# Head stage of a two-layer graph kernel: tap steps, forward transforms, statistics and norms put in another order, the last block's second sums moved to VectorE

## The chip, the cores and the metric

The kernel runs on one core of a Trainium2 chip. The metric is the device time of one execution in microseconds. The engines of the core run side by side, each through its own list of instructions: TensorE (PE in the profile, its weight loads PEld), VectorE (DVE), ScalarE (ACT), GpSimd (POOL) and SyncE (SP), which here only issues DMAs.

## The reference, cut to what matters

Two graph layers act on 128 graphs of 128 nodes with 256 channels, in float32. The stage that the change touches computes the first convolution path of layer 0: layer norm, ReLU, a 1x1 convolution (conv1), and the first half of a 17-tap convolution (conv2) over the node axis.

```python
# layer 0
h = jnp.maximum(_layernorm(x, axis=-1), 0.0)
x = x + _L0_gnn_ref(h, adj, L0_gnn_w_se, L0_gnn_b_se, L0_gnn_conv1_w)
...
def _L0_gnn_ref(x, mask, w_se, b_se, conv1_w):
    xc = jnp.transpose(x, (0, 2, 1))
    h = _bn(_conv1d(xc, conv1_w, 0), bn1_g, bn1_b, bn1_m, bn1_v)
    h = jax.nn.relu(h)
    h = _bn(_conv1d(h, conv2_w, 8), bn2_g, bn2_b, bn2_m, bn2_v)
    x_conv = jnp.transpose(jax.nn.relu(h + xc), (0, 2, 1))
    s = x @ w_se.T + b_se
    sq = jnp.sum(s * s, axis=-1)
    dist = sq[:, :, None] + sq[:, None, :] - 2.0 * jnp.einsum('bnd,bmd->bnm', s, s)
    A = jnp.exp(-dist) * mask
    msg = jax.nn.relu(x @ w_msg.T + b_msg)
    x_nmp = jnp.einsum('bnm,bmd->bnd', A, msg)
    ...
```

(The argument lists are shortened.) Behind it come a GRU cell on `x_conv`, `x_nmp` and x, and layer 1: two graph convolutions on each of five groups of nodes, added up.

## The kernel before

Conv2 is done in the frequency domain. The 128 graphs are dealt into 32 blocks (`NBLK`) of four (`BB`). The program has three stages. The **head stage** (about 0 to 254 us of the span) transforms conv2's taps and, block by block, conv1's output. The **spectral stage** (to about 430 us) multiplies the two spectra, 68 frequencies. The rest, nearly 1400 us, does the inverse transform, the message passing, the gates and layer 1.

The head stage runs under a manual schedule: on every engine the instructions stand in the order in which the Python code calls them. The later stages are ordered by the framework's planner. The pieces of the head stage, with their lines:

- `head_load(i)` (L198): SP issues the DMA of block i of x into a tile `ln`, of which there are four. It is called for block i+4 at the start of iteration i.
- `head_stats(i, parts)` (L208, L209, L212, L214): VectorE takes mean and variance of two graphs a part, by two bn_stats and two bn_aggr; behind the second part it adds the epsilon, and GpSimd takes the power of -1/2 into `rs`.
- `head_norm(i, wk, on_act)` (L221, L224, L227): VectorE makes `nm` = -mean x rs, then ScalarE normalises the first `on_act` graphs of the block in place, VectorE the others.
- `head_turn(i)` (L237, L238, L239): TensorE transposes the block, eight transposes into two PSUM banks; ScalarE applies ReLU into the tile `ht`, 512 columns at a time; SP writes `ht` to DRAM (`htd`).
- `head_conv1(i, h)` (L251, L254): one half of conv1 of a block, four matmuls of 128x256 (eight records in the trace) into one bank; VectorE evicts it with the batch norm's shift as a maximum, into `h1`.
- `head_sums(i, h)` (L261 to L263): GpSimd's sum and difference of two mirrored halves of the nodes, and an added constant: even and odd part, for a shorter transform.
- `head_spectra(X, i)` (L279, L288, L290): the forward transform of a block: TensorE in tiles of 64x64 into four banks; ScalarE and VectorE copy two banks each into `X`.
- a **tap step** (`between()`, which is `some_spectra`, one chunk of `weight_spectra`; L180, L187, L189): TensorE multiplies taps with the transform's matrix, in row tiles of 17, for two or three columns into four banks; ScalarE copies three or four of the banks, VectorE the fourth where the chunk has three columns. A set of taps has three chunks, 16 sets are done. Behind each set SP writes its spectrum to DRAM (L191, `vd<-sp`) and loads the taps after the next (L166, `w<-in_w2t_dram`); these two are issued at the call that begins the next set.

PSUM's eight banks are taken in turn: each new use waits until what stood there eight uses before has been evicted.

`heads` (L293 on) is the loop over the blocks. An odd iteration has two tap steps, an even one has one, so a pair of blocks does one set of taps, and the write of a spectrum falls on the second tap step of each odd iteration. SP's order in such a pair is: htd of an odd iteration, `vd<-sp`, taps, x of the next but three; then, in the even iteration, htd and x.

Of the kernel before, what the change touches and what calls it, by code (L numbers as in the profile page):

```python
# [10 lines left out]
ALU = mybir.AluOpType  # L11
# [6 lines left out]
BB = 4  # L18
# [57 lines left out]
def gnn_kernel(ctx: ExitStack, tc: tile.TileContext, io, out0: bass.AP, out1: bass.AP):  # L76
    nc = tc.nc
    x, adjT = io["x"], io["adjT"]
    NBLK, N, _, D = x.shape
# [11 lines left out]
    def bank():  # L91
        pool, n = banks
        if n is None:
            return pool.tile([P, 512], F32, tag="bank", name="bank")
        banks[1] = (n + 1) % 8
        return pool.tile([P, 512], F32, tag=f"bank{n}", name="bank")
# [17 lines left out]
    sh1x2, nsh1 = bnr[:, 0, :], bnr[:, 1, :]  # L114
# [81 lines left out]
    def head_load(pool, ahead, i, queue):  # L196
        xs[i] = pool.tile([P, BB, D], F32, tag="ln", name="ln", bufs=ahead)
        queue.dma_start(xs[i], x[i])  # L198

    def head_stats(wk, i, parts=(0, 1)):  # L200

        for h in parts:
            if not h:
                stats[i] = (wk.tile([P, BB, 2], F32, tag="mv", name="mv", bufs=3),
                            wk.tile([P, BB, 6], F32, tag="st", name="st", bufs=2))
            mv, st = stats[i]
            for b in range(h * BB // 2, (h + 1) * BB // 2):
                nc.vector.bn_stats(st[:, b, :], xs[i][:, b, :])  # L208
                nc.vector.bn_aggr(mv[:, b, :], st[:, b, :])  # L209
            if h:  # L210
                ve = wk.tile([P, BB], F32, tag="ve", name="ve", bufs=2)
                nc.vector.tensor_scalar(ve, mv[:, :, 1], EPS, None, op0=ALU.add)  # L212
                rs = wk.tile([P, BB], F32, tag="rs", name="rs", bufs=3)
                nc.gpsimd.tensor_tensor(rs, ve, mhalf, op=ALU.pow)  # L214
                stats[i] = mv, rs

    def head_norm(i, wk=None, on_act=BB):
        mv, rs = stats.pop(i)
        if wk is not None:
            nm = wk.tile([P, BB], F32, tag="nm", name="nm", bufs=2)  # L220
            nc.vector.scalar_tensor_tensor(nm, mv[:, :, 0], -1.0, rs, op0=ALU.mult, op1=ALU.mult)  # L221
        for b in range(BB):
            if wk is not None and b < on_act:
                nc.scalar.activation(xs[i][:, b, :], xs[i][:, b, :], AF.Identity, bias=nm[:, b:b + 1],  # L224
                                     scale=rs[:, b:b + 1])
                continue
            nc.vector.tensor_scalar(xs[i][:, b, :], xs[i][:, b, :], mv[:, b, 0:1], rs[:, b:b + 1],  # L227
                                    op0=ALU.subtract, op1=ALU.mult)

    def head_turn(wk, i):  # L230

        ln = xs.pop(i)
        ht = wk.tile([P, C, T], F32, tag="ht", name="ht", bufs=2)
        for c in range(C):
            ps = bank()
            for b in range(BB):
                nc.tensor.transpose(ps[:, b * N:(b + 1) * N], ln[:, b, c * P:(c + 1) * P], ident)  # L237
            nc.scalar.activation(ht[:, c, :], ps, AF.Relu)  # L238
        nc.sync.dma_start(htd[i], ht)  # L239
        hcs[i] = ht  # L240

    def head_conv1(wk, i, h):

        if not h:
            h1s[i] = wk.tile([P, BB, D], F32, tag="h1", name="h1", bufs=2)
        ht = hcs[i]
        ps = bank()
        pv = ps.rearrange("p (s d) -> p s d", s=2)
        for s in range(2):
            for c in range(C):  # L250
                nc.tensor.matmul(pv[:, s, :], ht[:, c, (2 * h + s) * N:(2 * h + s + 1) * N], wc1[:, c, :],  # L251
                                 start=c == 0, stop=c == C - 1)
        hv = h1s[i][:, 2 * h:2 * h + 2, :]
        nc.vector.tensor_tensor(hv, pv, nsh1[:, None, :].to_broadcast([P, 2, D]), op=ALU.max)  # L254

    def head_sums(ep, i, h):
        if not h:
            evens[i] = ep.tile([P, 2, D], F32, tag="ev", name="ev", bufs=2)
        lo, hi = h1s[i][:, 2 * h, :], h1s[i][:, 2 * h + 1, :]
        ev = evens[i][:, h, :]  # L260
        nc.gpsimd.tensor_tensor(ev, hi, lo, op=ALU.add)  # L261
        nc.gpsimd.tensor_tensor(hi, hi, lo, op=ALU.subtract)
        nc.gpsimd.tensor_tensor(ev, ev, sh1x2, op=ALU.add)  # L263

    def head_spectra(X, i):

        h1, ev = h1s.pop(i), evens.pop(i)
        g = slice(i * BB, (i + 1) * BB)
        for c in range(C):
            ps = [bank() for _ in range(2)]  # L270
            for h in range(BB // 2):
                for e in range(2):
                    c0 = (2 * h + e) * NP_
                    u = h1[:, 2 * h + 1, :] if e else ev[:, h, :]
                    for bb in range(2):
                        r = slice(64 * bb, 64 * bb + 64)
                        for q in range(2):
                            o = c * P + 64 * q
                            nc.tensor.matmul(ps[bb][64 * q:64 * q + 64, c0:c0 + NP_], u[r, o:o + 64], fd[r, e, :],  # L279
                                             start=True, stop=True)  # L280
            for bb in range(2):
                sv = ps[bb][:, :4 * NP_].rearrange("p (h e k) -> p k e h", h=2, e=2)
                d0 = 0
                for xt in X:
                    n = xt.shape[2]
                    to = xt[:, c, :, :, g].rearrange("p k e (h b) -> p k e h b", h=2)[:, :, :, :, bb]
                    if bb:
                        nc.vector.tensor_copy(to, sv[:, d0:d0 + n])  # L288
                    else:
                        nc.scalar.copy(to, sv[:, d0:d0 + n])  # L290
                    d0 += n

    def heads(wk, xk, ep, ahead, X, between, consts):  # L293

        for i in range(NBLK + 1):
            if i + ahead < NBLK:
                head_load(xk, ahead, i + ahead, nc.sync)
            if i < NBLK:
                head_conv1(wk, i, 0)
            between()  # L300
            if i and i % 2 == 0:
                head_spectra(X, i - 1)
            if i < NBLK:
                head_sums(ep, i, 0)
            if i == 0:
                head_norm(1, wk)
            elif i + 3 < NBLK:
                head_stats(wk, i + 3, (0,))
            if i < NBLK:
                head_conv1(wk, i, 1)  # L310
            if i + 1 < NBLK:
                head_turn(wk, i + 1)
            if i < NBLK:
                head_sums(ep, i, 1)
            if i == 0:
                head_stats(wk, 2)
            if i % 2 or i == 0:
                between()
            if i == 0:
                head_norm(2, wk)  # L320
            if i % 2:
                head_spectra(X, i - 1)
            if i and i + 2 < NBLK:
                head_norm(i + 2, wk, BB // 2)
            if i + 3 < NBLK:
                head_stats(wk, i + 3, (1,) if i else (0, 1))
            if i == 2:
                next(consts)

# [71 lines left out]
    with front as es:  # L401
# [8 lines left out]
        X = X0, X1  # L410
        with ExitStack() as ws:
# [48 lines left out]
            head_stats(hk, 1)  # L460
            some_spectra()
            heads(hk, xk, wp, ahead, X, some_spectra, consts)
            while spectra or todo:
                some_spectra()
# [41 lines left out]
    wk = ctx.enter_context(tc.tile_pool(name="wk", bufs=1, reuse_waits="tile"))  # L506
# [797 lines left out]
```

## Time and profile before

| what | us |
|---|---|
| median of three runs | 1837.84 (1836.28 to 1840.7) |
| the profiled execution's own time | 1838.96 |
| its span | 1837.1 |
| TensorE busy in the span | 1810.6 |
| conv1 matmuls, busy (L251, 512 records) | 128.2 |
| first spectral matmul starts at | 253.55 |
| head stage (0 to 254): PE, DVE, ACT, POOL busy | 241.15, 193.99, 160.64, 174.73 |
| head stage: busy share of the DMA engines, what they moved | 0.85, 318 GB/s |
| spectral stage (254 to 430): PE busy; share of the DMA engines | 175.91; 0.93 |

In a group or a timeline, `out<-in` are the program's tile names; L followed by a number is the line of the kernel. In a timeline the columns are start, duration, engine, line, operation, tiles and count, and in square brackets the engine's idle time just before with what ended it. In a list of waits the columns are the total in us, how often, and the longest. A matmul's end is modelled by the profiler, so the order and the starts of TensorE's weight loads are better guides than its busy share.

### The profile page before, as it was taken

Reading aid. Unit: us, or ns where it says so; the run is one execution under the profiler, and the core shown is the slowest. Engines: PE = TensorE matmul, PEld = TensorE weight load, DVE = VectorE, ACT = ScalarE, POOL = GpSimd, SP = SyncE. Lnnn points to the kernel's source line nnn. Section 1 sums busy time; section 2 is a strip of 40 time slices with the busy share of each in tenths; the row PEclk is TensorE's granted clock in tenths of the full one; section 3 lists DMA queues with packets and bytes.
Section 4 is the critical chain, followed back from the end, with each engine's and each line's share of the span. In section 5 each row is a group of like instructions: output and inputs, shape, how many; then the busy total and the mean of one; then the engine's idle time right before and its main releaser. Section 6 shows DMA issues by size and latency. Waiting matters only on the chain.

```text
span 1837.1 us, 34667 instructions
## 1 busy us (share of the span) xinstructions
PE 1810.6 (99%) x12552; PEld 1563.7 (85%) x12552; DVE 1357.2 (74%) x3328; ACT 734.4 (40%) x1624; POOL 790.5 (43%) x996
## 2 busy tenths in 40 slices
PE   8999999999999999999999999999999999999998
PEld 7777778887888888888788888888788888888786
DVE  7887857787878787877665787878656687877553
ACT  6666631112433434343434434333343434343343
POOL 5767775774344434443221344344312234443100
PEclk9999999999999999999999999999999999999999
DMA  8888889997533333343253433334334533342133
GB/s 302 330 326 326 330 292 309 350 309 228 146 83 74 85 84 78 86 108 91 63 114 102 121 85 85 74 82 115 79 82 97 140 71 90 79 101 50 42 94 119
DMA packets 279869, 267.46 MB, mean 146 GB/s; under 512 B 170870, under 2 KB 247371, under 8 KB 277651
## 3 DMA queue, kind: packets, MB, share of 16 engines
q1 hardware_dynamic: 274515, 247.32, 46.5%
q10 hardware_dynamic: 5184, 17.93, 2.4%
q8 instruction: 100, 1.64, 0.4%
q14 instruction: 70, 0.57, 0.1%
HBM read 168.84 MB, written 96.35 MB: 144 GB/s over the span
## 4 chain that ended last, share of the span: by engine, by line
PE 86%; DVE 4%; DMA 3%; issue 2%; ACT 2%; SPq 1%; POOL 1%; DVEq 0%; ACTq 0%
PE bank L708 44%; PE bank L365 6%; PE bank L1035 5%; PE bank L976 5%; PE bank L609 5%; PE bank L251 4%; PE bank L360 3%; PE bank L659 3%; PE bank L588 3%; PE bank L180 2%; PE bank L955 1%; DMA nt<-in_adjN_dram 1%; PE bank L885 1%; PE bank L279 1%; PE bank L237 1%
## 5 line engine op out<-in xcount | busy, mean ns | idle before, releaser
L721 POOL TENSOR_TENSOR u<-u,m 128x256 f32<-128x256 f32 x128 | 94.1, 735 | 461.7 <-ACT m L719 420.1
L708 PE MATMUL bank<-t,sw 128*128 128x256 f32 x1152 | 292.0, 380 | 0.7 <-DVE nn L723 0.4
L708 PEld LDWEIGHTS bank<-t,sw 128*128 128x128 f32 x1152 | 215.1, 191 | 33.5 <-issue 3.0
L708 PE MATMUL bank<-t,wih 128*128 128x256 f32 x768 | 200.3, 383 | 0.0
L708 PEld LDWEIGHTS bank<-t,wih 128*128 128x128 f32 x768 | 143.2, 190 | 29.3 <-DVE o L748 6.6
L251 PE MATMUL bank<-wc,ht 128*128 128x256 f32 x512 | 128.2, 394 | 4.8 <-ACT ht L238 4.8
L357 POOL TENSOR_TENSOR vs<-v 128x256 f32<-128x256 f32 x134 | 101.7, 783 | 52.7 <-DMA v<-vd 30.9
L708 PE MATMUL bank<-xc,wih 128*128 128x256 f32 x384 | 115.3, 382 | 1.6 <-ACT xc L592 1.6
L708 PE MATMUL bank<-xn,wih 128*128 128x256 f32 x384 | 114.9, 381 | 0.0
L1035 PE MATMUL bank<-w,hh 128*125 128x256 f32 (+9 forms) x480 | 114.6, 382 | 0.1
L708 PE MATMUL bank<-t,whh 128*128 128x256 f32 x384 | 114.6, 380 | 0.1
L251 PEld LDWEIGHTS bank<-wc,ht 128*128 128x128 f32 x512 | 90.8, 189 | 25.0 <-ACT ht L238 11.2
L708 PE MATMUL bank<-ht,whh 128*128 128x256 f32 x384 | 110.5, 381 | 0.7 <-DVE msg L628 0.4
L632 ACT ACTIVATE msg<-msg 128x512 f32<-128x512 f32 x64 | 36.8, 621 | 184.2 <-DVE msg L628 184.2
L592 ACT ACTIVATE xc<-xc,bn 128x512 f32<-128x512 f32 x64 | 46.2, 722 | 154.2 <-DVE xc L591 154.2
L1035 PEld LDWEIGHTS bank<-w,hh 128*125 128x125 f32 (+9 forms) x480 | 85.2, 179 | 18.5 <-DVE hh L981 1.2
L976 PE MATMUL bank<-ax,w 128*128 128x500 f32 (+9 forms) x352 | 94.5, 404 | 1.4 <-DVE xc L591 1.3
L726 DVE TENSOR_TENSOR u<-bank,u 128x256 f32<-128x256 f32 x128 | 53.3, 416 | 49.1 <-PE bank L708 48.6
L362 ACT COPY k<-bank 128x256 f32<-128x256 f32 x67 | 24.9, 372 | 145.8 <-PE bank L360 71.7
L708 PEld LDWEIGHTS bank<-xc,wih 128*128 128x128 f32 x384 | 72.3, 191 | 11.7 <-ACT xc L592 2.2
L189 ACT COPY sp<-bank 128x408 f32<-128x408 f32 (+1 forms) x160 | 66.9, 506 | 37.7 <-PE bank L180 37.5
L708 PEld LDWEIGHTS bank<-xn,wih 128*128 128x128 f32 x384 | 73.2, 191 | 10.1
(221 smaller groups left out, 4535.4 us busy)
## 6 DMA issues: line engine op xcount, KB each, us to landing
vd<-sp SPq DMA_DIRECT2D x16, 2176.0 KB
v<-vd SPq DMA_DIRECT2D x34, 1024.0 KB
w<-in_w_dram SPq DMA_DIRECT2D x40, 512.0 KB
ln<-in_x_dram SPq DMA_DIRECT2D x32, 512.0 KB
htd<-ht SPq DMA_DIRECT2D x32, 512.0 KB
yd<-ys ACTq DMA_DIRECT2D x32, 512.0 KB
ht<-htd SPq DMA_DIRECT2D x64, 256.0 KB
ym<-yd SPq DMA_DIRECT2D x32, 512.0 KB
```

Of the source, the lines that this page charges most:

```text
L189: nc.scalar.copy(dst, s)
L251: nc.tensor.matmul(pv[:, s, :], ht[:, c, (2 * h + s) * N:(2 * h + s + 1) * N], wc1[:, c, :], start=c == 0, stop=c == C - 1)
L357: nc.gpsimd.tensor_tensor(vs[:, c], vi[c], vr[c], op=ALU.subtract)
L360: nc.tensor.matmul(p1[:, :D], a[:, c], vs[:, c], start=c == 0, stop=c == C - 1)
L365: nc.tensor.matmul(ps[:, k * D:(k + 1) * D], u[:, c], w[c], start=c == 0, stop=c == C - 1)
L588: nc.tensor.matmul(ps[:, b * N:(b + 1) * N], ym[:, 2 * h + b, o * P:(o + 1) * P], idm, start=False, stop=b == 1)
L609: nc.tensor.matmul(ps[:, b, :], d[:, b * N:(b + 1) * N], w, start=True, stop=True)
L659: nc.tensor.matmul(ps[:, b * N:(b + 1) * N], msg[:, b, c * P:(c + 1) * P], e[:, b, :], start=True, stop=True)
L708: nc.tensor.matmul(ps, w, d, start=n == 0, stop=n == len(pairs) - 1)
L721: nc.gpsimd.tensor_tensor(got["u4"], got["u2"], got["m5"], op=ALU.add)
L976: nc.tensor.matmul(pv[:, q - q0, :], w1s[k5 + g][:, c, q * P:(q + 1) * P], xv[:, c], start=c == 0, stop=c == C - 1)
L1035: nc.tensor.matmul(ps[:n1, :D], hh[:, q, at:at + n1], w2s[k5 + g][:, q, :], start=q == 0, stop=q == HID // P - 1)
```

## The change

`heads` deals out the same calls in another order, from iteration 1 on. Iteration 0 is now written out by itself, with the calls and the order that it had. In the iterations behind it:

- `head_stats(i+3, (0,))` stands ahead of the block's first half of conv1 (before: behind it), and `head_stats(i+3, (1,))` directly behind the second half, ahead of the transposes (before: last in the iteration);
- `head_norm(i+2)` stands between the first sums and the second half of conv1 (before: behind the transposes and the second sums);
- the even iteration's tap step and the forward transform of block i-1 stand behind the transposes of block i+1 (before: between the halves of conv1); in odd iterations they stood there already;
- the three sums of the last block's second half are done by VectorE instead of GpSimd.

```diff
--- before.py
+++ after.py
@@ -258,9 +258,10 @@
             evens[i] = ep.tile([P, 2, D], F32, tag="ev", name="ev", bufs=2)
         lo, hi = h1s[i][:, 2 * h, :], h1s[i][:, 2 * h + 1, :]
         ev = evens[i][:, h, :]
-        nc.gpsimd.tensor_tensor(ev, hi, lo, op=ALU.add)
-        nc.gpsimd.tensor_tensor(hi, hi, lo, op=ALU.subtract)
-        nc.gpsimd.tensor_tensor(ev, ev, sh1x2, op=ALU.add)
+        eng = nc.vector if h and i == NBLK - 1 else nc.gpsimd
+        eng.tensor_tensor(ev, hi, lo, op=ALU.add)
+        eng.tensor_tensor(hi, hi, lo, op=ALU.subtract)
+        eng.tensor_tensor(ev, ev, sh1x2, op=ALU.add)
 
     def head_spectra(X, i):
 
@@ -293,37 +294,42 @@
     def heads(wk, xk, ep, ahead, X, between, consts):
 
         for i in range(NBLK + 1):
+            more = i < NBLK
             if i + ahead < NBLK:
                 head_load(xk, ahead, i + ahead, nc.sync)
-            if i < NBLK:
+            if i == 0:
+                head_conv1(wk, 0, 0)
+                between()
+                head_sums(ep, 0, 0)
+                head_norm(1, wk)
+                head_conv1(wk, 0, 1)
+                head_turn(wk, 1)
+                head_sums(ep, 0, 1)
+                head_stats(wk, 2)
+                between()
+                head_norm(2, wk)
+                head_stats(wk, 3)
+                continue
+            if i + 3 < NBLK:
+                head_stats(wk, i + 3, (0,))
+            if more:
                 head_conv1(wk, i, 0)
-            between()
-            if i and i % 2 == 0:
-                head_spectra(X, i - 1)
-            if i < NBLK:
+            if i % 2:
+                between()
+            if more:
                 head_sums(ep, i, 0)
-            if i == 0:
-                head_norm(1, wk)
-            elif i + 3 < NBLK:
-                head_stats(wk, i + 3, (0,))
-            if i < NBLK:
+            if i + 2 < NBLK:
+                head_norm(i + 2, wk, BB // 2)
+            if more:
                 head_conv1(wk, i, 1)
+            if i + 3 < NBLK:
+                head_stats(wk, i + 3, (1,))
             if i + 1 < NBLK:
                 head_turn(wk, i + 1)
-            if i < NBLK:
+            if more:
                 head_sums(ep, i, 1)
-            if i == 0:
-                head_stats(wk, 2)
-            if i % 2 or i == 0:
-                between()
-            if i == 0:
-                head_norm(2, wk)
-            if i % 2:
-                head_spectra(X, i - 1)
-            if i and i + 2 < NBLK:
-                head_norm(i + 2, wk, BB // 2)
-            if i + 3 < NBLK:
-                head_stats(wk, i + 3, (1,) if i else (0, 1))
+            between()
+            head_spectra(X, i - 1)
             if i == 2:
                 next(consts)
```

`more` is true while the block i exists. What each called function does is unchanged but for `head_sums`.

## The prediction

> **What bounds the kernel now.** I read the page first: TensorE is busy all through, so only a stage in which it stalls can give time. The diff touches the head stage alone, the first 254 us, so I asked next for that stage's windows and waits.
>
> ```profile
> PE 1810.6 (99%) x12552; PEld 1563.7 (85%) x12552; DVE 1357.2 (74%) x3328; ACT 734.4 (40%) x1624; POOL 790.5 (43%) x996
> ```
> ```profile
> 52.95:232.30 179.35, 174.44 (x2880) 142.32 (x2880) 144.01 (x458) 117.43 (x314) 128.58 (x169) 1.00 0.86 325
> ```
> The window covers twelve pairs of blocks (i odd, then even): 179.35 / 12 = 14.95 us a pair. Columns are PE, PEld, DVE, ACT, POOL, clock, DMA share, GB/s. The DMA engines are 86% busy and DVE 80%: a faster PE order has little room on either. The waits in 50 to 236 us:
>
> ```profile
> PEld bank L180 <- issue: 9.5, 32, 0.3
> PEld bank L251 <- ACT ht L238: 9.5, 26, 0.5
> PEld bank L279 <- DVE h L254: 2.6, 9, 0.6
> ```
> ```profile
> DVE st L208 <- DMA ln<-in_x_dram: 18.2, 11, 2.6
> ```
> PE waits mostly at tap steps (L180) and, once a pair, for `ht` right behind the transposes. VectorE's statistics wait eleven times for x to land. The timeline shows why: SP's queue, then VectorE and ScalarE, in block 25 (odd, conv1 from 202.78).
>
> ```profile
> 194.49 0.33 SPq L239 DMA_DIRECT2D htd<-ht  x1
> 194.91 0.38 SPq L191 DMA_DIRECT2D vd<-sp  x1
> 195.39 0.74 SPq L166 DMA_DIRECT2D w<-in_w2t_dram  x1
> 196.23 1.13 SPq L198 DMA_DIRECT2D ln<-in_x_dram  x1
> 203.24 0.33 SPq L239 DMA_DIRECT2D htd<-ht  x1
> 203.67 0.64 SPq L198 DMA_DIRECT2D ln<-in_x_dram  x1
> 209.07 0.33 SPq L239 DMA_DIRECT2D htd<-ht  x1
> 209.49 0.38 SPq L191 DMA_DIRECT2D vd<-sp  x1
> ```
> ```profile
> 207.40 0.43 DVE L208 BATCH_NORM_STATS2 st<-ln 128x6 f32<-128x256 f32 x1 [1.83 <-DMA ln<-in_x_dram]
> ...
> 208.48 0.66 DVE L254 TENSOR_TENSOR h<-bank,bnr 128x512 f32<-128x512 f32 x1
> ...
> 210.84 0.62 DVE L221 SCALAR_TENSOR_TENSOR nm<-mv,rs 128x4 f32<-128x4 f32 x1
> ```
> ```profile
> 207.96 1.09 ACT L238 ACTIVATE ht<-bank 128x512 f32<-128x512 f32 x2 [1.16 <-issue]
> ...
> 211.50 1.09 ACT L224 ACTIVATE ln<-ln,nm,rs 128x256 f32<-128x256 f32 x2 [0.23 <-DVE nm L221]
> ```
> ```profile
> 195.00:202.00 7.00, 7.00 (x162) 5.98 (x153) 6.54 (x24) 4.92 (x16) 4.15 (x6) 1.00 1.05 394
> 202.00:203.00 1.00, 0.70 (x6) 0.46 (x5) 1.00 (x4) 0.87 (x2) 0.58 (x1) 1.00 0.46 156
> ```
> Once a pair `vd<-sp` (2176 KB), the next taps (512 KB) and one x block (512 KB) enter SP's queue together. The statistics of that x block start 12.5 us after the vd issue (194.91 to 207.40). All eleven waits, each from its vd issue: 12.41 to 13.27, mean 12.68 us. In the window at 202 fewer than half of the DMA engines still work, before the next transfer is issued: the slowest engines set the landing.
>
> **What the Trainium skill says.** "TensorE: Matmul & The Clock Gate", section "Architectural detail: the array is 16× 32×32, not 1× 128×128": ScalarE and VectorE are strict FIFO. The trace agrees: both ran every line above in program order, VectorE standing 1.83 us at the statistics with conv1's eviction behind them. "DMA: Bandwidth & Descriptors", section "Queues, rings and completion order": each DMA engine consumes its descriptors in ring order; the 12.68 us fit, as x lands behind vd and taps though issued over 11 us before. "TensorEngine Tiling (Array Packing)", section "Key Properties": changing the tiling mode drains TensorE. The trace agrees: a tap step behind conv1 starts 0.33 us late, behind transposes 0.17.
>
> **The change part by part.**
>
> *PE's order.* Write C for a half of conv1, H for the transposes, T for a tap step, S for the forward transforms. Before: odd C T C H T S, even C T S C H, and the next C needs the `ht` just transposed. After: odd C T C H T S, even C C H T S. From starts of weight loads: C to T 1.92 (210.29 to 212.21), T of two columns 0.67, C to H 1.62, H to T 1.18, T of three columns 0.90, S 1.15, C to C 1.60 (eight loads of 0.2). The new pair: odd 1.92+0.67+1.62+1.18+0.90+1.15 = 7.44; even 1.60+1.62+1.18+0.90+1.15 = 6.45; together 13.9 us. What goes is the wait for `ht` (0.54+0.19) and a stall of S on conv1's late eviction (some 0.25 to 0.4). If nothing else bound, 1.1 us a pair. The same matmuls, evictions, sums and DMAs are issued as before.
>
> *Statistics ahead of conv1's halves, norm ahead of the transposes.* This builds a loop that was not there. Before, `ht`'s relu (L238) came ahead of the next norm on ScalarE, so htd, and with it vd, taps and x on SP, never waited for these statistics. After, in an odd iteration: statistics(i+3) are first on VectorE and wait for x; behind them queue conv1's eviction, then nm; ScalarE's norm(i+2) waits for nm; the relus of turn(i+1) queue behind that norm; SP's htd waits for the relus; vd, taps and x(i+5) queue behind htd; and x(i+5) is what statistics wait for one pair later. From landing to the next vd issue: two statistics with their aggregates 1.08 (207.40 to 208.48), eviction 0.66, nm 0.3 (0.15 alone, 0.62 beside GpSimd's sums; between, as sums start then too), to ScalarE 0.04, two norms 1.09, two relus 1.09, to SP 0.03, htd to vd 0.42: 4.71 us. Plus 12.68 from vd to landing: **17.4 us a pair**, against 13.9 that PE would need. Tap step and transforms behind the transposes cannot start either: their PSUM banks come free with that eviction and those relus. The `ht` wait that goes is replaced by this one, about 3.5 us a pair of PE standing still.
>
> *How many.* The loop runs from the vd issue of iteration 3 (44.26) to that of 27 (224.53): twelve pairs, 15.02 us each before. 12 x (17.39 - 15.02) = +28.4.
>
> *Start.* In iteration 1 statistics(4) go ahead of the first eviction, and norm(3), two activations on ScalarE, ahead of the relus. VectorE is through with statistics(3) at 25.6; then 1.08, eviction 0.66, nm 0.2, norms 1.1, relus 1.1 give htd at 29.9 where it was 28.07. The vd issue of iteration 1 moves from 28.49 to 30.3, that of iteration 3 to 30.3+12.68+4.71 = 47.7: +3.4. Iteration 0 is unchanged: the same calls in the same order.
>
> *End.* Iteration 29 has no statistics left: its pair runs at 13.9 against 14.57: -0.7. The last sums: GpSimd's three (0.73 each, queued behind the first half's, which end at 250.26) end at 252.46 and PE waits 1.84 us for them. VectorE's three are not in the trace; its plain 128x256 adds there take 0.43, up to 0.73 if each yields to GpSimd: 1.3 to 2.2 us from 249.67, done by 251 to 251.9. But SP's v loads come behind the last vd, still landing then (SP waits 2.4 us for it), and PE's first spectral product starts at 253.55 for v that landed about 252.5. I take -1.0; bounds 0 and -1.9.
>
> *Sum.* 28.4+3.4-0.7-1.0 = +30.1. The profiled execution took 1838.96 us (span 1837.1), 1.1 above the median of 1837.84: 1868 us as a median. After the head stage nothing is edited; the order there is a planner's and may shift by one or two us, which I leave in the range.
>
> **The unknown costs.** Vd to landing: no better than 3277 KB (the three transfers in units of 1000 bytes) at 394 GB/s, 8.3, plus the 2.0 us fixed part that "DMA: Bandwidth & Descriptors" gives in "Anatomy of one DMA" (for another issue path, and no run here isolates it, so an estimate) = 10.3; no worse than the 13.27 seen. I take 12.68, since the DMA engines stand idle before each vd issue already (share 0.12 in 208 to 210), so the delay is no backlog that more time would drain. The path to vd: 4.5 (nm 0.15) to 5.0 (0.62). With 11.5 (halfway) and 4.6 a pair is 16.1 and the total +14; with 13.3 and 5.0 it is 18.3 and +42. The likeliest case alone: 1852 to 1880.
>
> **Rivals.**
> - *Landing sooner.* The queue has fewer neighbours when pairs are longer, so x lands 10.3 to 11.5 us after vd. For: the slow engines' tail at 202 may come from mixing. Against: all eleven landings are beyond 12.4. Pairs of 15.0 to 16.1 us, +1 to +14: about 1846.
> - *Faster: the loop does not bind.* Then PE sets 13.9, 14 pairs x 1.1 and the end's 1.0 give -16: 1821. The mechanism is the hidden `ht` relu, between H and C. It decides once landing takes under 13.9-4.7 = 9.2 us; break-even is 15.02-4.71 = 10.3. For: PE's waits in the page are real and the edit removes them. Against: no landing comes near.
> - *PE's clock falls as well.* PE would be idle some 3.5 us of 17.4. the granted clock was 0.91 in the window of 240 to 260, where it stalled at the stage's end. If a third of each pair's 13.9 ran slower, most would hide in the stall; 1 us a pair more gives 1882.
>
> **Chances.** 0.67 the loop as computed (1868), 0.15 landing sooner (0.10 slower, 0.05 within the bound), 0.13 faster, 0.05 the clock (slower). A measurement of this kernel tells 0.2%, 3.7 us, from no change. Faster 0.13, same 0.05, slower 0.82. The range 1842 to 1882 leaves out the faster case and the ends.
>
> **What would show it.** Right: VectorE's L208 waits for ln some 4 to 5 us in each odd iteration, 60 us in all; vd issues 17 us apart; ScalarE's L224 waits for nm, with L238 behind; PE waits at L180 and L279 on VectorE and ScalarE. The `ht` wait before L251 (9.5) gone shows the first part alone. Wrong: vd issues 14 us apart, or statistics starting without a wait.

## The result and the profile after

The changed kernel takes 1869.39 us (median of five runs, 1867.69 to 1871.27), the kernel before 1839.81 us (five runs, 1836.28 to 1841.61): a ratio of 1.0165, 95% interval 1.015 to 1.018. It is slower by some 30 us. The profiled execution took 1868.6 us, its span is 1866.8.

The page first: the busy time of the engines, the granted clock and the DMA share over forty slices, then the chain that ended last by engine and by line. (Line numbers behind the edit are larger by up to six: L708 is now L714, L279 is L280.)

```profile
PE 1824.8 (98%) x12552; PEld 1581.5 (85%) x12552; DVE 1359.8 (73%) x3331; ACT 732.3 (39%) x1624; POOL 790.4 (42%) x993
...
PEclk9899999999999999999999999999999999999999
DMA  7777769998733333334324433334333433332134
...
PE 82%; DMA 9%; DVE 4%; POOL 1%; SPq 1%; issue 1%; ACT 0%; DVEq 0%; ACTq 0%; POOLq 0%
PE bank L714 43%; DMA ln<-in_x_dram 7%; PE bank L371 6%; PE bank L1041 5%; PE bank L982 5%; PE bank L615 5%; PE bank L366 3%; PE bank L665 3%; PE bank L594 3%; PE bank L251 3%; PE bank L280 1%; PE bank L961 1%; PE bank L891 1%; DMA nt<-in_adjN_dram 1%; PE bank L571 1%
```

In the kernel before the DMA row was:

```profile
DMA  8888889997533333343253433334334533342133
```

The first six slices fell from 8 to mostly 7: the head stage moves the same bytes in more time. In the chain a DMA, the load of x, is the second costliest line, 7% of 1866.8 us, about 130 us. Its transfers are 512 KB each; the chain shows that they are waited for, one after another, not that one of them is slow. Who waits, over 20 to 300 us of the changed kernel (total us, times, longest), for VectorE, PE's weight loads, ScalarE:

```profile
DVE st L208 <- DMA ln<-in_x_dram: 47.0, 13, 5.5
```
```profile
PEld bank L180 <- DVE h L254: 21.0, 11, 3.9
```
```profile
ACT ln L224 <- DVE nm L221: 76.4, 27, 5.2
```

Thirteen waits for x, one in each odd iteration from 3 to 27, 3.6 us each; PE waits at the tap step for VectorE's eviction. The wait of L251 for `ht`, 9.5 us before, is gone, as the edit meant. One turn of the loop in the timeline, from x landing to the queue that the next x stands in: VectorE, then PE's tap step, ScalarE, SP (start, duration).

```profile
202.14 0.43 DVE L208 BATCH_NORM_STATS2 st<-ln 128x6 f32<-128x256 f32 x1 [4.18 <-DMA ln<-in_x_dram]
...
203.23 0.67 DVE L254 TENSOR_TENSOR h<-bank,bnr 128x512 f32<-128x512 f32 x1
203.82 0.15 DVE L221 SCALAR_TENSOR_TENSOR nm<-mv,rs 128x4 f32<-128x4 f32 x1
...
203.95 0.78 PEld L180 LDWEIGHTS bank<-gt,w 17*128 17x128 f32 x24 [2.14 <-DVE h L254]
...
204.01 1.09 ACT L224 ACTIVATE ln<-ln,nm,rs 128x256 f32<-128x256 f32 x2 [3.54 <-DVE nm L221]
...
205.01 1.06 ACT L238 ACTIVATE ht<-bank 128x512 f32<-128x512 f32 x2
```
```profile
206.09 0.33 SPq L239 DMA_DIRECT2D htd<-ht  x1
206.51 0.39 SPq L191 DMA_DIRECT2D vd<-sp  x1
206.99 0.74 SPq L166 DMA_DIRECT2D w<-in_w2t_dram  x1
207.82 1.17 SPq L198 DMA_DIRECT2D ln<-in_x_dram  x1
```
```profile
219.96 0.43 DVE L208 BATCH_NORM_STATS2 st<-ln 128x6 f32<-128x256 f32 x1 [4.34 <-DMA ln<-in_x_dram]
```

Read it as a ring (the loop of the prediction): x landed (202.14), statistics, eviction, nm, norm, relus, htd, vd issue (206.51), 4.37 us; and from there 13.45 us until the next x has landed (219.96). The transposes of that iteration had ended on PE at 202.06; in the kernel before their relus would have run at once.

### The profile page after: what moved, and what is told of

Same layout as the page of the kernel before. It is cut to its first block, busy times and chain, and to the rows that moved or that the text cites. A ratio compares the mean times of both kernels' runs of the same rounds, so it can differ in the third digit from the quotient of the medians.

```text
span 1866.8 us, 34711 instructions
## 1 busy us (share of the span) xinstructions
PE 1824.8 (98%) x12552; PEld 1581.5 (85%) x12552; DVE 1359.8 (73%) x3331; ACT 732.3 (39%) x1624; POOL 790.4 (42%) x993
## 4 chain that ended last, share of the span: by engine, by line
PE 82%; DMA 9%; DVE 4%; POOL 1%; SPq 1%; issue 1%; ACT 0%; DVEq 0%; ACTq 0%; POOLq 0%
PE bank L714 43%; DMA ln<-in_x_dram 7%; PE bank L371 6%; PE bank L1041 5%; PE bank L982 5%; PE bank L615 5%; PE bank L366 3%; PE bank L665 3%; PE bank L594 3%; PE bank L251 3%; PE bank L280 1%; PE bank L961 1%; PE bank L891 1%; DMA nt<-in_adjN_dram 1%; PE bank L571 1%
## 5 line engine op out<-in xcount | busy, mean ns | idle before, releaser
L714 PE MATMUL bank<-t,sw 128*128 128x256 f32 x1152 | 291.9, 380 | 0.8 <-POOL t L689 0.4
L714 PEld LDWEIGHTS bank<-t,sw 128*128 128x128 f32 x1152 | 215.0, 191 | 33.4 <-issue 2.8
L714 PE MATMUL bank<-t,wih 128*128 128x256 f32 x768 | 200.3, 384 | 0.0
L714 PEld LDWEIGHTS bank<-t,wih 128*128 128x128 f32 x768 | 143.5, 190 | 29.0 <-DVE o L754 6.6
L251 PE MATMUL bank<-wc,ht 128*128 128x256 f32 x512 | 134.9, 416 | 0.0
L251 PEld LDWEIGHTS bank<-wc,ht 128*128 128x128 f32 x512 | 101.8, 207 | 18.7
L714 PE MATMUL bank<-xc,wih 128*128 128x256 f32 x384 | 114.9, 381 | 0.9 <-ACT xc L598 0.8
L714 PE MATMUL bank<-t,whh 128*128 128x256 f32 x384 | 114.7, 380 | 0.1
L714 PE MATMUL bank<-xn,wih 128*128 128x256 f32 x384 | 114.3, 379 | 0.0
L714 PE MATMUL bank<-ht,whh 128*128 128x256 f32 x384 | 110.3, 381 | 0.3 <-DVE m L625 0.3
L208 DVE BATCH_NORM_STATS2 st<-ln 128x6 f32<-128x256 f32 x128 | 51.8, 405 | 51.1 <-DMA ln<-in_x_dram 51.1
L714 PEld LDWEIGHTS bank<-xn,wih 128*128 128x128 f32 x384 | 73.1, 190 | 9.8
L714 PEld LDWEIGHTS bank<-xc,wih 128*128 128x128 f32 x384 | 72.2, 191 | 10.5 <-ACT xc L598 1.4
```

The source lines that it names most:

```text
L714: nc.tensor.matmul(ps, w, d, start=n == 0, stop=n == len(pairs) - 1)
```

## The experiments

All are variants of one loop, `heads`. "Vd to vd" is the mean distance of SP's `vd<-sp` issues from iteration 3 to 27, twelve pairs of blocks; "landing" is the mean from a vd issue to the start of the statistics that waited for x behind it. It counts only those turns in which the statistics did wait. Both come from the timelines of SP and VectorE, so from the one profiled execution of each kernel; the medians are those of all its runs. (The profiled execution of e10 is the slowest of four, 1859.4 us, those of e3 and e4 are faster than the median, 1860.3 and 1833.8 us.) The runs of the kernel before were repeated beside each group of experiments, and the ratios are to those. PE needs 13.9 us a pair by the prediction's count.

| kernel | vd to vd, us | landing, us | median us | ratio to before, 95% |
|---|---|---|---|---|
| before | 15.02 | 12.68 | 1837.4 to 1840.5 | |
| changed | 17.45 | 13.10 | 1869.4 | 1.0165 (1.015 to 1.018) |
| both moves of statistics and norm alone (e5) | 17.09 | 12.68 | 1869.5 | 1.0166 (1.0149 to 1.0183) |
| PE's order alone (e4) | 14.75 | 13.25 | 1837.4 | 0.9988 (0.9971 to 1.0006) |
| changed, statistics behind norm (e1) | 15.17 | 13.44 | 1844.9 | 1.0029 (1.0017 to 1.0041) |
| changed, statistics behind conv1, ahead of norm (e2) | 16.91 | 13.22 | 1863.7 | 1.0138 (1.0116 to 1.0159) |
| changed, norm behind transposes (e3) | 16.54 | 13.16 | 1863.1 | 1.0132 (1.0109 to 1.0155) |
| changed, norm last (e10) | 16.48 | 13.57 | 1851.8 | 1.0064 (1.004 to 1.0089) |
| changed, taps behind x in the queue (e9) | 16.17 | 11.76 | 1857.1 | 1.0089 (1.0075 to 1.0103) |
| changed, x ahead of vd in the queue (e6) | 14.14 | no wait | 1828.2 | 0.9947 (0.993 to 0.9964) |
| PE's order alone, x ahead (e7) | 14.40 | no wait | 1826.3 | 0.9939 (0.9924 to 0.9954) |
| before, x ahead (e8) | 14.65 | no wait | 1833.0 | 0.9974 (0.996 to 0.9988) |

### The two parts apart

Statistics and norm as changed, PE's order as before:

```diff
-            if i % 2:
-                between()
+            between()
+            if i % 2 == 0:
+                head_spectra(X, i - 1)
             if more:
                 head_sums(ep, i, 0)
...
-            between()
-            head_spectra(X, i - 1)
+            if i % 2:
+                between()
+                head_spectra(X, i - 1)
```

> The other part alone: statistics ahead of conv1's halves and norm ahead of the transposes as in the changed kernel, with TensorE's order of the kernel before. Theory: the loop is there in full and sets the pair whatever PE's order: 17.3 to 17.6 us, time about 1869 (1862 to 1875). Rival 1: without the new PE order about 1840. Rival 2: about 1840, since the traffic was carried in 15 us a pair before.

Measured: 1869.5 us, the whole loss of the change, with PE's old order; 17.09 us a pair, a little under what was expected. So the loss comes with the moves of statistics and norm. PE's order adds 0.36 us a pair to it (17.45 against 17.09), which is the later landing of x (13.10 against 12.68); in the medians that doesn't show.

The other part, statistics and norm back where they were:

```diff
             if more:
                 head_sums(ep, i, 0)
+            if i + 3 < NBLK:
+                head_stats(wk, i + 3, (0,))
...
             head_spectra(X, i - 1)
+            if i + 2 < NBLK:
+                head_norm(i + 2, wk, BB // 2)
+            if i + 3 < NBLK:
+                head_stats(wk, i + 3, (1,))
```

> The changed kernel's order on TensorE and its last sums by VectorE, with statistics and norm where the kernel before has them. Theory: no loop; the wait for ht goes, the second half's eviction behind the statistics costs some 0.5 us: 14 to 14.6 us a pair, time about 1831 (1823 to 1838), with no PEld wait of L251 on ht. Rival 1: this is the part that costs, so about 1869. Rival 2: not faster than the kernel before, 1840 or more.

Measured: 1837.4 us, the same as before within the interval, where 1831 was expected. The wait for `ht` is gone here too, yet a pair takes 14.75 us, not 13.9. Waits in 45 to 240 us of this kernel:

```profile
PEld bank L280 <- DVE h L254: 5.9, 10, 1.0
```
```profile
DVE st L208 <- DMA ln<-in_x_dram: 12.7, 12, 1.5
```

A pair was expected at 14.6 us at most. The forward transform (L280) waits for conv1's second eviction, which stands behind the statistics, which wait for x. With PE's order better, the next thing late was x again; e7, further down, tests that.

### Cutting the ring at the statistics and at the norm

The first half of the statistics behind the norm (in e2, behind `head_conv1(wk, i, 0)` instead):

```diff
-            if i + 3 < NBLK:
-                head_stats(wk, i + 3, (0,))
...
             if i + 2 < NBLK:
                 head_norm(i + 2, wk, BB // 2)
+            if i + 3 < NBLK:
+                head_stats(wk, i + 3, (0,))
```

> The changed kernel, but the first half of the statistics stands behind the norm instead of ahead of conv1's first half; nothing else moves. Theory (loop: x lands, statistics, eviction, nm, norm on ScalarE, relus, htd, vd issue, x lands 13 us later): the loop is cut, because nm no longer queues behind the statistics. Vd issues come 14 to 14.6 us apart instead of 17.45 (the second half's eviction still queues behind the statistics, and the forward transform needs its bank: some 0.5 us over PE's 13.9), time about 1831 (1823 to 1836). Rival 1 (PE's new order and its PSUM banks are what costs): the order is unchanged, so about 1869. Rival 2 (the DMA engines cannot carry the traffic faster): about 1869 too.

Measured: 15.17 us a pair and 1844.9 us. The ring is cut, as 24 of the 30 us are gone, but 1831 was missed by 14. Part of it is that x lands later than the 13.0 us that I had put in (13.44 here): the statistics still wait for it, and the forward transform waits 11.6 us for evictions of conv1 in 45 to 240 us. That is at most 0.44 us a pair; 15.17 us is 0.57 above the upper end of what was expected, so a part of the gap is not resolved.

> The changed kernel with the first half of the statistics moved behind conv1's first half, but still ahead of the norm. Theory: of the loop's path from landing to the next vd issue (4.40 us measured) only the eviction (0.67 us) goes, the rest stays: 17.45 - 0.67 = 16.8 us a pair, time about 1861 (1856 to 1865). If the eviction's wait for PE's banks were the cost, and not the norm behind the statistics, the time would fall to 1845 or less.

Measured: 16.91 us a pair, 0.54 less than the changed kernel, and 1863.7 us. Taking one eviction of 0.67 us out of the ring shortened each turn by about that eviction (from landing to vd most turns take 3.77 us, 0.6 less than the 4.37 above). With e1 this sets the norm behind the statistics apart from the eviction behind them.

The norm behind the transposes and second sums, statistics left ahead:

```diff
-            if i + 2 < NBLK:
-                head_norm(i + 2, wk, BB // 2)
...
             if more:
                 head_sums(ep, i, 1)
+            if i + 2 < NBLK:
+                head_norm(i + 2, wk, BB // 2)
             between()
```

> The changed kernel, but the norm stands behind the transposes and the second sums again; the statistics stay ahead of conv1's halves. Theory: the relus no longer queue behind nm, so vd is issued in PE's time; what is left is the eviction of conv1's first half behind the statistics, whose bank the tap step needs: it starts 1.75 us after x has landed. Worked out over two pairs that is 14.9 to 15 us a pair, time about 1838 (1832 to 1845). Rival 1 and rival 2: about 1869, since PE's order and the traffic are those of the changed kernel.

Measured: 1863.1 us, a clear miss. Its timeline, ScalarE and then PE (one odd iteration):

```profile
195.86 1.09 ACT L224 ACTIVATE ln<-ln,nm,rs 128x256 f32<-128x256 f32 x2 [1.09 <-DVE nm L221]
196.86 1.28 ACT L189 COPY sp<-bank 128x408 f32<-128x408 f32 x3
...
197.39 3.32 PEld L251 LDWEIGHTS bank<-wc,ht 128*128 128x128 f32 x16 [1.48 <-ACT sp L189]
```

The norm is out of the relus' way, but it now stands on ScalarE ahead of the tap step's copies (L189), still waiting for nm; conv1 of the next block needs the bank of the first of these copies. Over 45 to 240 us the weight loads of L251 waited 31.5 us for them (24 times, twice a pair), 2.6 us a pair; with PE's 13.9 that is the 16.5 us measured. I had overlooked what else queues behind a waiting instruction. Moving the norm behind copies and transform tests that:

```diff
             head_spectra(X, i - 1)
+            if i + 2 < NBLK:
+                head_norm(i + 2, wk, BB // 2)
```

> The changed kernel with the norm last in each iteration, behind tap step and forward transform (statistics stay ahead of conv1's halves). The run with the norm directly behind the transposes took 1863 where 1838 was expected. Theory: there the norm, waiting for nm, stood ahead of ScalarE's copies of the tap step, so conv1 of the next block waited for their banks; with the norm behind these copies only the eviction behind the statistics is left: about 15 us a pair, time about 1840 (1834 to 1846). If it is the statistics ahead of the eviction that cost 1863, this stays at 1860 or more.

Measured: 1851.8 us (1846.25 to 1859.39), a second miss, between the two cases: the copies were worth 11 us of the first. Its pairs are not alike, they alternate between 13.95 and about 20 us. A pair that isn't held issues vd early, the pair behind it asks early for an x that has not landed. Windows of a short pair, a long one, the wait in it and what follows (PE, PEld, DVE, ACT, POOL busy, clock, DMA share, GB/s):

```profile
160.75:174.70 13.95, 12.77 (x210) 10.77 (x200) 9.86 (x28) 9.72 (x26) 8.75 (x11) 1.00 0.97 344
174.70:194.77 20.07, 18.44 (x284) 15.55 (x288) 16.32 (x50) 10.21 (x27) 13.04 (x17) 0.83 0.68 249
173.00:176.30 3.30, 0.52 (x5) 0.28 (x3) 1.72 (x6) 1.09 (x2) 0.00 (x0) 1.00 0.91 359
176.30:180.00 3.70, 3.67 (x89) 3.29 (x90) 3.21 (x10) 1.84 (x7) 3.40 (x5) 0.55 0.96 401
180.00:184.00 4.00, 4.00 (x11) 3.23 (x12) 2.92 (x10) 1.44 (x4) 2.06 (x3) 0.56 0.98 321
```

PE stood still for 3.04 us before 176.33, and over the next 7.7 us its granted clock averaged 0.55: sixteen weight loads of conv1 took 5.14 us there and 3.32 in the short pair. The long pair is 13.9 + 2.9 of waiting + 3.2, and the clock is the likeliest cause of the last term (7.7 us at 0.55 are 3.5 us of work less than at 1.00); no run was made that changes the clock alone.

### The queue

If x lands late because of what stands ahead of it in SP's queue, a change of that order alone must change the time. The dose first: the next taps' load is issued behind the x load instead of ahead of it; the spectrum's write stays ahead.

```diff
                         if len(todo) > 1:
-                            taps.append(taps_load(wp, *todo[1], nc.sync))
+                            later.append(todo[1])
...
                 head_load(xk, ahead, i + ahead, nc.sync)
+            load_later()
             if i == 0:
```

(`load_later` issues the held load.)

> The changed kernel with the next taps (512 KB) loaded behind the x block instead of ahead of it; the spectrum's write (2176 KB) stays ahead of x. A dose for the queue's term: if SP's queue is served in order, x lands sooner by what the taps take, 524 KB at the 394 GB/s of the full windows = 1.3 us: vd to landing 11.8 instead of 13.1, 16.1 us a pair instead of 17.45, time about 1853 (1848 to 1858). If all transfers in flight share the engines, whatever their order, x lands when all have: no change, about 1869.

Measured: landing 11.76 us where 11.8 was expected, 16.17 us a pair where 16.1 was, 1857.1 us. What stands ahead of x in the queue delays it: these 512 KB were worth 1.3 us a pair. That the queue is served strictly in order is not shown. In the changed kernel 4.70 MB moved (339 GB/s) from the htd issue at 206.09 us to the start of the statistics at 219.96, and htd, vd, taps and x are 3.80 MB together: 0.9 MB of what was issued behind x had moved as well. Either later transfers overtake in part, or the word that x has landed comes late, by up to the 2.7 us that 0.9 MB take at 339 GB/s; the runs don't tell which.

Then x ahead of both:

```diff
-            if i + ahead < NBLK:
+            if (i < 2 or i % 2) and i + ahead < NBLK:
                 head_load(xk, ahead, i + ahead, nc.sync)
...
             if more:
                 head_sums(ep, i, 1)
+            if i % 2 and i + 1 + ahead < NBLK:
+                head_load(xk, ahead, i + 1 + ahead, nc.sync)
             between()
```

> The changed kernel with one DMA issued earlier: in odd iterations the x load of the next iteration is put ahead of the tap step, so it stands ahead of the spectrum's write and the taps in SP's queue instead of behind them. Bytes, engines' orders and matmuls are unchanged. Theory: x then lands behind half a megabyte of htd and itself only, long before the statistics ask for it; the loop of 17.45 us is gone and PE's own 13.9 to 14.2 us a pair shows, time about 1825 (1818 to 1831). Rival 2 (the DMA engines cannot carry the traffic faster than it comes now): the time stays near 1869, the wait only moves to another tile. Rival 1 (PE's order and banks): near 1869.

Measured: 1828.2 us, ratio 0.9947 (0.993 to 0.9964): the changed kernel with one load issued some 1.7 us earlier beats the kernel before. SP's queue in an odd iteration, and PE, DVE, ACT, POOL, clock, DMA share and GB/s over 50 to 230 us:

```profile
173.11 0.33 SPq L239 DMA_DIRECT2D htd<-ht  x1
173.54 0.37 SPq L198 DMA_DIRECT2D ln<-in_x_dram  x1
174.01 0.98 SPq L191 DMA_DIRECT2D vd<-sp  x1
175.04 0.43 SPq L166 DMA_DIRECT2D w<-in_w2t_dram  x1
```
```profile
50.00:230.00 180.00, 177.51 (x3067) 150.77 (x3069) 155.49 (x475) 125.84 (x332) 138.93 (x180) 1.00 0.89 340
```

The same engines carry 340 GB/s here and 280 in the changed kernel, so traffic as such was never the limit of the changed kernel. PE is busy 177.51 of 180 us, its clock is full.

> TensorE's new order with statistics and norm where the kernel before has them (14.75 us a pair when run by itself, where the forward transform waited for conv1's second eviction behind statistics that waited for x), now with the x load ahead of the spectrum's write in SP's queue. Theory: that wait goes, and the pair falls to 14.0 (13.9 to 14.3): time about 1826 (1819 to 1831). If the traffic itself bounds the stage, nothing is gained over 1837.

Measured: 1826.3 us, 14.40 us a pair: the new PE order with statistics and norm left alone, and x ahead, is the fastest seen (0.9939, 0.9924 to 0.9954). The time was hit, the pair not: 14.3 us at most was expected, and what holds the rest is open. It is 1.9 us below e6 although its pairs are longer. In the profiled executions (1828.0 and 1828.5 us) the head stage is 1.4 us longer than in e6 and the part behind it 1.9 us shorter, so the two orders are not told apart.

> The kernel before with the same one DMA issued earlier. Theory: only the stall of the forward transform on conv1's late eviction goes (2.6 us of PEld over twelve pairs in the trace of before, and what follows from it); the wait for ht stays. Pairs of 14.7 to 14.95 us, time 1833 to 1838, about 1836.

Measured: 1833.0 us (0.9974, 0.996 to 0.9988), 14.65 us a pair. The old order had a little of the same wait; the early load takes it out. The same move of one load is worth some 41 us to the changed kernel and some 4 to the kernel before, so it isn't a gain that any order would have had: it is mostly what the ring cost.

### The last block's sums

The e6 kernel with `eng = nc.gpsimd` for all blocks:

> The fastest form of the changed kernel (x load ahead of the spectrum's write, 1828 us) with the last block's second sums back on GpSimd: what the sums by VectorE are worth. Expected: 1828 to 1829, a difference below 1.5 us, since the first spectral product also waits for v to land; the trace should show PE's first spectral load as long after the last spectrum's write (14.5 us) as with VectorE, or up to 1.5 us later.

Measured: 1829.3 us, ratio 0.9944 (0.993 to 0.9957). From the last vd issue to PE's first spectral weight load are 14.58 us here and 14.48 with VectorE: nothing. PE waits for the sums with GpSimd and for v (1.9 us) with VectorE, so the end of the stage stays where v lands.

## Why the prediction was right

**What bounds the stage.** The ring was found before the run from one fact of the trace of before (statistics standing 12.41 to 13.27 us behind the vd issue) and the program order on three in-order queues, VectorE, ScalarE, SP. The experiments bear out the links: e5 shows that the two moves alone make the loss, e1 that it is the statistics ahead of nm, e2 one eviction in the ring, e9 one transfer ahead in the queue, e6 that the ring goes with x's place in the queue. The link from norm to relus on ScalarE is read from the timeline alone: e3 and e10 take it out, but bring waits of their own. Two signs came smaller than foretold: the waits for x are 3.6 us and 47.0 in all, not 4 to 5 and 60, and PE stands idle 1.6 us a pair, not 3.5, because at its lower clock it takes longer for the same work (see the rivals).

**12 x (17.39 - 15.02) = +28.4.** Measured 17.45, so +29.1. Inside it two sizes were off and cancelled: landing is 13.10 (13.05 over these twelve turns), not 12.68, and landing to vd 4.40, not 4.71. The second is that successive rows overlap by some 0.1 us each and that nm took 0.15, not 0.3. The first comes with PE's new order: with the old one (e5) landing is 12.68 as in the kernel before. What in the new order delays x was not tried. The traces point at the transfers that follow: over the eight kernels with vd and taps ahead of x, x lands on the whole later the sooner the next htd is issued behind vd. On average htd comes 8.7 and 9.0 us behind vd where landing is 12.68 (before, e5), 6.6 to 7.8 where it is 13.1 to 13.4, and 6.1 where it is 13.57 (e10). No run changes that alone. The distance between pairs doesn't order them: 12.68 was seen at 15.02 and at 17.09 us a pair. One reading was wrong here: the prediction took the low DMA share at 202 us (0.46) as the slowest engines setting x's landing. From 203 us to the landing at 207.4 the share is 1.00 at 396 GB/s, so x's landing is not the end of that lull.

**Start, +3.4.** Measured +5.6 at the vd issue of iteration 3 (49.87 against 44.26). Of that 1.9 stand already at the first vd issue (17.31 against 15.44), in an iteration that the edit leaves as it was; in the other runs that issue lies anywhere between 15.5 and 17.3, so it is scatter. The rest, 3.7, is the term.

**End, -0.7 and -1.0.** The last pair gave -0.8. The sums gave nothing: 14.58 us from last vd to first spectral load against 14.45. The prediction had seen v's landing about a microsecond ahead of that load and still counted a gain of one; v lands later by what the sums save.

**The total, +30.1.** The head stage in fact grew by 34.05 us (first spectral load at 287.60 instead of 253.55), of which 1.9 is the scatter above. The part behind it, whose instructions stand in the same order in both programs (but for one small GpSimd instruction at its start), took 1579.2 us from that load to the end of the span, against 1583.5; over the thirteen profiled kernels of this study it lies between 1579.2 and 1585.8. So the prediction's 1868 came closer to 1869 than its terms were right: the head grew by 4 us more than they say, half of it the scatter, and 4.3 us were given back by chance behind it. That the sum came within 1.5 us is luck; the mechanism is not.

**The rivals.** "Landing sooner" fell: it was later. "Faster: the loop doesn't bind" fell, but its 13.9 us is real: e6 reaches 14.14. "PE's clock falls as well" was right in what happens: over 50 to 259.4 us of the changed kernel the clock is 0.91, and in the window behind one wait 0.50:

```profile
50.00:259.40 209.40, 189.94 (x2898) 158.36 (x2892) 147.21 (x457) 115.81 (x313) 129.80 (x168) 0.91 0.77 280
...
224.00:226.00 2.00, 2.00 (x52) 1.78 (x46) 1.93 (x10) 1.78 (x7) 1.31 (x3) 0.50 0.64 260
```

It cost nothing visible here, as PE, which needs 13.9 us of a turn of 17.45, has time to spare; in e10, where PE sets every other pair, it is the likeliest reason for 3 us.

**What the edit was worth without the ring.** The prediction priced PE's order at 1.1 us a pair if nothing else bound. Alone (e4) it brought 0.27, because x bound next. With x out of the way it has to be compared with the kernel before that has its x early too (e8, 14.65 us a pair): PE's order alone is then worth 0.25 us a pair (e7, 14.40) and 6.7 us of time, the whole edit 0.51 us a pair (e6, 14.14) and 4.8 us. So about half of the 1.1 is the most that was seen, and moving statistics and norm brought no time at all: e6 is not faster than e7.

## What to carry to other kernels

Before an instruction that waits for a DMA is moved forward in an in-order queue, follow what queues behind it, over all queues, until you come to an end or back to that DMA; if you come back, the time of one turn is the sum of the links, and no engine's busy share told it here. Order loads within one DMA queue by when their readers need them: a small load that is waited for goes ahead of a large write that nobody awaits. And a part of an edit that seems to bring nothing (e4) can be held by the same wait that makes another part slower.

## What the hardware showed that was not expected

- After some 3.0 us without work PE's granted clock averaged 0.55 over 7.7 us (e10), more than twice the length of the pause. In the changed kernel, behind a wait of 2.1 us at the tap step (201.8 to 203.95), the clock was 0.62 from 206.8 to 211 us, and conv1's sixteen weight loads took 4.86 us instead of the 3.32 of e10's short pair.
- The landing of one x block behind the same transfers took 12.7 us with one order of the other engines and 13.1 to 13.6 with another, on the whole later the sooner the next write was issued behind it.
